# Routing of a four-batch chunk cut into pieces, rows normed ahead of the copy, and, in the last part, reciprocal roots on VectorE and an expert product behind the transposes

## Chip, core and metric

One core of a Trainium2 chip runs the whole program in one launch. The metric is device time in microseconds (us), the median over runs of the same program. PE is TensorE, PEld its weight loads, DVE is VectorE, ACT is ScalarE, POOL is GpSimd, SP is SyncE; SP, ACT and POOL also issue DMAs.

## What is computed

Inputs are x (64 batches of 256 rows of 256 floats), one 256x256 adjacency matrix, and the weights of two layers. All is float32.

```python
x = x + elu(attention_of_4_heads(layernorm(x), adj, W0, a0))   # _L0_gnn_ref
x = x + layernorm(x) @ weight.T + bias                          # _L0_ffn_ref
x = x + relu(attention_of_1_head(layernorm(x), adj, W1, a1))   # _L1_gnn_ref
x = x + moe(layernorm(x))                                       # _L1_ffn_ref: 8 experts, the best 2 of each row
```

In `_moe` the eight logits of a row choose two experts and two weights; the result is the normed row itself plus, for both experts, weight x (gelu(row @ w1 + b1) @ w2 + b2). `_layernorm` needs one reciprocal root per row; there are four norms.

## The kernel before

Each batch is one Python generator, `batch_layers`, with two tiles of 128 rows (`NT` = 2). The order of the instructions on every engine is written out by hand: a loop over *ticks* (`step`) at the end of the kernel resumes every live generator once per tick, in the order of the rank that it gave with `yield` the last time (lower first); a negative rank means "go on in this same tick at that rank". A new batch starts every third tick (`TICKS` = 3), so a tick has a phase 0, 1 or 2, about six batches are in flight, and the engines see in each phase a fixed mix of stages of different batches. All engines run their own queue in order.

In the first 61 batches (`ROUTED`) the expert layer is routed. `CHUNKS` has twelve chunks of four batches, then five of two and three of one; the last three batches are dense (all eight experts). When the last batch of a chunk has its logits (`pl`, L701, rank 35 in phase 2), `route` runs for the chunk: `top_two` (the two best experts, 13 small DVE operations with `m`, L1026), a pair of tiny matmuls that count rows ahead (`pp`, L1034 and L1035), a scan and positions (`both` to `pos`, L1037 to L1063), the two weights (L755 to L758), and then one tick after another the indirect DMAs that send each row to its place (`send`, L1000, on POOL, two per tick), with `allot` between them, which hands out pairs of tiles to experts. `later` waits for a phase. After the last send the chunk's pairs are put in `waiting`.

A *pair* (`expert_pair`) is 256 rows of one expert: loads (`xr`, `xt`, `we`), a transpose on DVE (`sT`, L117), `hidden` (`ph`, L892 on PE, then Gelu, L898 on ACT), `result` (`py`, L907 on PE, then L917 on DVE), a scaling (L885 on ACT), and two indirect DMAs that add the rows to the output (`scatter`, L928, on POOL). Up to the tick `DRAIN_AT` = 3 x 59 = 177 two pairs are begun in phase 1 of every batch; from there on (batch 59 starts) one pair per tick.

Norms: `norm_stats` (DVE, L375 and L376; the norms of x0 and x1) and `norm_squares` (ACT, L402; the two norms of x2) give variances; `finish_norms` and `finish_squares` take the root for up to four columns at once with two POOL operations, an add (L383, L412) and a power (L384, L415). The norm ahead of the experts makes `by` on DVE (L659, L662) in phase 0, rank 8, from the root of the tick before; then, at rank 50, ACT writes the normed rows `xng` (L671) and `base` (L676). `xng` is turned by PE (`pt`, L421) at rank 55 of phase 1 for the logits. `transposed` is four PE transposes and one ACT copy (`xT`, L427). Ranks that matter below: phase 0: 20 `projected1` (`pq`, L472), 22 `projected` (L437), 30 `transposed(x1)`, 31 an ACT-queue DMA (L579) that waits for a DVE transpose; phase 1: 25 `scores1` (`pd`, L491), 50 `attended` (`pv`, L544), 70 `pf` (L618) and x2 (L625); phase 2: 7 `norm_squares(x2)`, 30 a pair's `hidden`, 35 `pl`, 36 `transposed(x2)`, 40 `attended` of the single head.

Of the kernel before, what the change touches and what calls it, by code (L numbers as in the profile page):

```python
# [27 lines left out]
def kernel(  # L28
# [17 lines left out]
    nc = tc.nc  # L46
    B, N, D = x.shape
# [311 lines left out]


    half_done = []

    def norm_stats(src):

# [13 lines left out]
            finish_norms(2 * NT)  # L378
        return mv[:, at : at + NT, :], rstd[:, at : at + NT]

    def finish_norms(n):
        mv, rstd = half_done.pop()
        nc.gpsimd.tensor_scalar_add(rstd[:, :n], mv[:, :n, 1], EPS)  # L383
        nc.gpsimd.tensor_tensor(rstd[:, :n], rstd[:, :n], mhalf[:, :n], ALU.pow)  # L384

# [4 lines left out]

    def norm_squares(src, sums):
        if half_squared:
            sq, rstd = half_squared[0]
            at = NT
        else:
            sq = small.tile([P, 2 * NT], F32, tag="sq", name="sq", bufs=4)
            rstd = small.tile([P, 2 * NT], F32, tag="rstd", name="rstd", bufs=5)
            half_squared.append((sq, rstd))
            at = 0
        for t in range(NT):  # L400
            off = work.tile([P, D], F32, tag="off", name="off", bufs=1)
            nc.scalar.activation(  # L402
                off, src[:, t, :], AF.Square, bias=sums[:, t : t + 1], scale=-float(D),
                accum_out=sq[:, at + t : at + t + 1],
            )
        if at:
            finish_squares(2 * NT)
        return rstd[:, at : at + NT]

    def finish_squares(n):  # L410
        sq, rstd = half_squared.pop()
        nc.gpsimd.tensor_scalar(  # L412
            rstd[:, :n], sq[:, :n], 1.0 / D**3, EPS, op0=ALU.mult, op1=ALU.add
        )
        nc.gpsimd.tensor_tensor(rstd[:, :n], rstd[:, :n], mhalf[:, :n], ALU.pow)  # L415
# [138 lines left out]
    def batch_layers(b, c0, xng, lg):  # L554
# [105 lines left out]
            by[:, 0], sums, -1.0 / D, rstd, op0=ALU.mult, op1=ALU.mult  # L660
        )
        nc.vector.tensor_scalar(by[:, 1], rstd, 1.0, None, op0=ALU.add)  # L662
        yield -50
        xe = keep.tile([P, NT, ROW], F32, tag="xng", name="xng", bufs=XNG)
        dense = b >= ROUTED
        base = (
# [3 lines left out]
        for t in range(NT):  # L670
            nc.scalar.activation(  # L671
                xe[:, t, :D], x2[:, t, :], AF.Identity, bias=by[:, 0, t : t + 1],
                scale=rstd[:, t : t + 1],
            )
        for t in range(NT):
            nc.scalar.activation(  # L676
                base[:, t, :], x2[:, t, :], AF.Identity, bias=by[:, 0, t : t + 1],
                scale=by[:, 1, t : t + 1],
            )
# [44 lines left out]
    def chunk_tile(shape, name, c, bufs=2, dt=F32):  # L724
        return keep.tile([P] + shape, dt, tag=name, name=f"{name}_{c}", bufs=bufs)

    def top_two(c, nt, lg, first):


        rt = lambda shape, name: chunk_tile(shape, name, c)  # L730
        vec, tt = nc.vector, nc.vector.tensor_tensor
        emb = em8[:, None, :].to_broadcast([P, nt, E])
        ohs, tops, lcur = rt([2, nt, E], "ohs"), [], lg
        for k in range(2):
            top = rt([nt], f"top{k}")
            vec.tensor_reduce(top, lcur, AX.X, ALU.max)
            eq = rt([nt, E], "eq")
            tt(eq, lcur, top[:, :, None].to_broadcast([P, nt, E]), ALU.is_equal)
            tt(eq, eq, emb, ALU.mult)

            least = rt([nt], "least") if k else first
            vec.tensor_reduce(least, eq, AX.X, ALU.min)
            oh = ohs[:, k]
            tt(oh, emb, least[:, :, None].to_broadcast([P, nt, E]), ALU.is_equal)
            if k == 0:
                lcur = rt([nt, E], "l2")
                vec.scalar_tensor_tensor(lcur, oh, -3.0e38, lg, op0=ALU.mult, op1=ALU.add)
            tops.append(top)
        ed = rt([nt], "ed")
        tt(ed, tops[1], tops[0], ALU.subtract)  # L750
        return ohs, ed

    def two_weights(less, second, ed):

# [15 lines left out]
    def allot(c, n, last):  # L770

        rt = lambda shape, name, bufs=2, dt=F32: chunk_tile(shape, name, c, bufs, dt)
        vec, tt = nc.vector, nc.vector.tensor_tensor
        full = rt([E], "full")
        vec.tensor_scalar(
            full, rows[0], 1.0 / PAIR, ((PAIR - 1.0 if last else 0.0) - (PAIR - 1.0) / 2) / PAIR,
            op0=ALU.mult, op1=ALU.add,
        )  # L780
        whole(full, full)
        wait = rt([E], "wait")
        tt(wait, full, used, ALU.subtract)
        ends = rt([E], "ends")
        vec.tensor_tensor_scan(ends, ones[:, :E], wait, 0.0, ALU.mult, ALU.add)
        start = rt([E], "start")
        tt(start, ends, wait, ALU.subtract)
        tt(shift[:, :E], used, start, ALU.subtract)
        took = rt([E], "took")
        vec.tensor_scalar(took, start, -1.0, float(n), op0=ALU.mult, op1=ALU.add)  # L790
        vec.scalar_tensor_tensor(took, took, 0.0, wait, op0=ALU.max, op1=ALU.min)
        tt(used, used, took, ALU.add)
        step = rt([E], "step")
        tt(step, shift[:, 1:], shift[:, :E], ALU.subtract)
        yield
        past = rt([n, E], "past")
        tt(
            past, ends[:, None, :].to_broadcast([P, n, E]),
            jrow[:, :n, None].to_broadcast([P, n, E]), ALU.is_le,
        )  # L800
        ef = rt([n], "ef", 8)
        vec.tensor_reduce(ef, past, AX.X, ALU.add)
        ids = rt([2, n], "ids", 8, I32)
        vec.tensor_scalar(ids[:, 0], ef, float(E - 1), None, op0=ALU.min)
        vec.tensor_scalar(ef, ef, float(E - 1), float(-E), op0=ALU.min, op1=ALU.add)
        tt(past, past, step[:, None, :].to_broadcast([P, n, E]), ALU.mult)
        pair_of = rt([n], "pair_of")
# [10 lines left out]
    def expert_pair(j, n, ids, ef, regs, needs):  # L818
# [46 lines left out]
        xT = turned(work.tile([P, KT, PAIR], F32, tag="sT", name="sT", bufs=3), xr)  # L865
        w = small.tile([P, 2], F32, tag="w", name="w", bufs=12)
        yield 30
        yield 30
        hT = hidden(xT, we)
        yield -65  # L870
        nc.vector.scalar_tensor_tensor(
# [121 lines left out]
        active.append([rank, len(order), job])  # L993
        order.append(job)

    order, order_steps = [], []

    def send(xe, at):

        d = nc.gpsimd.indirect_dma_start(  # L1000
# [10 lines left out]
    def later(rank, *phases):  # L1011

        yield rank
        while more and order_steps[-1] % TICKS not in phases:
            yield rank

    def route(c, row0, nt, n, last, xng, lg):

        rt = lambda shape, name, bufs=2, dt=F32: chunk_tile(shape, name, c, bufs, dt)
        vec, tt = nc.vector, nc.vector.tensor_tensor  # L1020
        yield -90

        tail = rt([nt, 3], "tail")
        ohs, ed = top_two(c, nt, lg, tail[:, :, 0])
        m = rt([E, nt], "m")
        tt(m.rearrange("p e t -> p t e"), ohs[:, 0], ohs[:, 1], ALU.add)  # L1026


        spread = nt == NTC
        yield from later(90, *((0,) if spread else (1, 2)))  # L1030

        mf = m.rearrange("p e t -> p (e t)")
        pp = bank("pp", [2, E, nt])
        nc.tensor.matmul(pp[:, 0].rearrange("p e t -> p (e t)"), tri, mf, start=True, stop=True)  # L1034
# [26 lines left out]
        vec.tensor_reduce(posf, ohs, AX.X, ALU.add)  # L1061
        pos = rt([2, nt], "pos", 4, I32)
        vec.tensor_copy(pos, posf)  # L1063
        yield from later(90, *((0,) if spread else (1, 2)))
        two_weights(tail[:, :, 1], tail[:, :, 2], ed)
        for i, xe in enumerate(xng):
            vec.tensor_copy(xe[:, :, D + 1 :], tail[:, i * NT : (i + 1) * NT, :])
        parts = allot(c, n, False)
        if n and not spread:
            next(parts)  # L1070
            ids, ef = next(parts)
        if last:
            ends_at = rt([E], "ends_at", 2, I32)
            vec.tensor_copy(ends_at, rows[0])
# [2 lines left out]
        for t in range(nt):  # L1077
            for k in range(2):
                send(xng[t // NT][:, t % NT, :], pos[:, k, t : t + 1])
            if n and spread and t in (1, 4):  # L1080
                ids, ef = next(parts) or (None, None)
            if not last:
                yield 95
            elif t % 2:
                yield 95
# [5 lines left out]
            )  # L1091
        if last:
            parts = allot(c + 1, FLUSH, True)
            next(parts)
            ids2, ef2 = next(parts)
# [23 lines left out]
    def route_dense(b, lg):  # L1119

        c = len(CHUNKS) + 1 + b - ROUTED
        ohs, ed = top_two(c, NT, lg, chunk_tile([NT], "first", c))
        yield 75
        nc.scalar.activation(ed, ed, AF.Exp)
        two = chunk_tile([2, NT], "two", c)
# [40 lines left out]
    step, more, credit = 2, True, 0.0  # L1166


    DRAIN_AT = TICKS * (B - 5)
    SETUP_AT = 4  # L1170
    dense_free = 0
    with tc.manual_schedule():
        while more or active or waiting or dense_jobs or scatters:
# [35 lines left out]
            if half_done:  # L1209
                finish_norms(NT)  # L1210
            if half_squared:
                finish_squares(NT)
            active[:] = [a for a in active if a[0] is not None]
            step += 1

# [34 lines left out]
```

## Time and profile before

| | |
|---|---|
| median of 3 runs | 1548.69 us (1545.79 to 1563.14) |
| the profiled execution | 1561.7 us, of which the span of the instructions is 1559.9 us |
| PE, PEld busy | 93%, 82% of the span |
| DVE, ACT, POOL busy | 80%, 65%, 56% |
| mean granted TensorE clock | 0.963 |

The span has three parts. Up to about 311 us there are batches but (almost) no pairs. From about 368 to 1068 us four batches and eight pairs together take 82 us. The last part starts with tick 177, at about 1140 us (first norm of batch 59); the last batch's first norm is at 1238.9 us, the routing of the last batches ends near 1400 us, and from there pairs and dense experts alternate on PE. A line of the view by windows gives, for one stretch of time, its length, the busy time and number of instructions of PE, PEld, DVE, ACT and POOL, the granted share of the PE clock, and the share and rate of the DMA engines. A line of the waits gives engine and line that waited, what ended the wait, the total us, how often, and the longest.

### The profile page before, as it was taken

Reading aid. Unit: us, or ns where it says so; the run is one execution under the profiler, and the core shown is the slowest. Engines: PE = TensorE matmul, PEld = TensorE weight load, DVE = VectorE, ACT = ScalarE, POOL = GpSimd, SP = SyncE. Lnnn points to the kernel's source line nnn. Section 1 sums busy time; section 2 is a strip of 40 time slices with the busy share of each in tenths; the row PEclk is TensorE's granted clock in tenths of the full one; section 3 lists DMA queues with packets and bytes.
Section 4 is the critical chain, followed back from the end, with each engine's and each line's share of the span. In section 5 each row is a group of like instructions: output and inputs, shape, how many; then the busy total and the mean of one; then the engine's idle time right before and its main releaser. Section 6 shows DMA issues by size and latency. Waiting matters only on the chain. (4 is left out here: it accounts for less than half of the span.)

```text
span 1559.9 us, 29960 instructions
## 1 busy us (share of the span) xinstructions
PE 1457.4 (93%) x8066; PEld 1283.5 (82%) x8066; DVE 1252.9 (80%) x4392; ACT 1006.7 (65%) x2381; POOL 878.1 (56%) x853
## 2 busy tenths in 40 slices
PE   7899998899999999999999999999898988869997
PEld 6688887788888989898989898888787867757886
DVE  7787879798898988888888888889888868545544
ACT  1365556577777777777777777766676778644332
POOL 2111435356666767575767575766764667644443
PEclk9888889899999999999999999999999999989999
DMA  5653333367777778777877777777677776788863
GB/s 148 201 150 90 110 104 109 108 171 156 184 173 171 171 164 181 164 181 157 193 163 184 161 179 164 169 160 183 156 168 165 146 159 126 148 192 157 158 106 46
DMA packets 372851, 240.83 MB, mean 154 GB/s; under 512 B 264772, under 2 KB 334924, under 8 KB 372684
## 3 DMA queue, kind: packets, MB, share of 16 engines
q1 hardware_dynamic: 311488, 138.31, 36.3%
q0 software_dynamic: 48864, 66.33, 23.5%
q10 hardware_dynamic: 12332, 34.28, 6.7%
q8 instruction: 66, 1.08, 0.3%
q14 instruction: 101, 0.83, 0.2%
HBM read 150.46 MB, written 88.35 MB: 153 GB/s over the span
## 5 line engine op out<-in xcount | busy, mean ns | idle before, releaser
L928 POOL DMA_INDIRECT out_dram<-y,xt x258 | 413.7, 1604 | 197.5 <-issue 69.3
L544 PE MATMUL pv<-q,z 128*128 128x65 f32 (+1 forms) x2560 | 375.7, 304 | 0.3
L544 PEld LDWEIGHTS pv<-q,z 128*128 128x128 f32 x2560 | 343.5, 200 | 12.9 <-DVE z L530 0.8
L1000 POOL DMA_INDIRECT xs<-xng,pos x244 | 260.0, 1065 | 65.7 <-issue 59.3
L907 PE MATMUL py<-w2s,hT 128*128 (+1 forms) x1224 | 287.6, 386 | 8.6 <-ACT hT L898 8.5
L907 PEld LDWEIGHTS py<-w2s,hT 128*128 128x128 f32 x1224 | 232.6, 194 | 42.8 <-ACT hT L898 11.7
L892 PE MATMUL ph<-sT,we 128*128 128x256 f32 x1032 | 242.0, 383 | 8.0 <-DMA we<-wpack 2.3
L530 DVE SCALAR_TENSOR_TENSOR z<-z,q,mask 128x256 f32<-128x256 f32 x504 | 232.3, 482 | 13.4 <-DMA z<-terms 4.4
L892 PEld LDWEIGHTS ph<-sT,we 128*128 128x128 f32 x1032 | 196.1, 192 | 38.6 <-PE ph L892 5.3
L671 ACT ACTIVATE xng<-x,by,rstd 128x256 f32<-128x256 f32 x128 | 69.8, 593 | 156.4 <-DVE stats L375 82.2
L898 ACT ACTIVATE hT<-ph,we 128x256 f32<-128x256 f32 x306 | 123.4, 472 | 64.4 <-PE ph L892 47.3
L885 ACT ACTIVATE y<-y,w 128x256 f32<-128x256 f32 x258 | 112.0, 497 | 80.9 <-DVE y L917 79.3
L383 POOL TENSOR_SCALAR rstd<-mv 128x4 f32<-128x4 f32 (+1 forms) x67 | 15.9, 238 | 252.5 <-DVE mv L376 200.5
L472 PE MATMUL pq<-wx,xT 128*128 128x259 f32 x512 | 129.2, 395 | 26.3 <-ACT xT L427 26.2
L427 ACT COPY xT<-pt 128x512 f32<-128x512 f32 x192 | 113.8, 592 | 43.4 <-PE pt L421 43.4
L402 ACT ACTIVATE off<-x,sums 128x256 f32<-128x256 f32 x256 | 129.4, 505 | 17.6 <-DVE x L625 11.9
L472 PEld LDWEIGHTS pq<-wx,xT 128*128 128x128 f32 x512 | 96.5, 194 | 53.2 <-ACT xT L427 39.4
L618 PE MATMUL pf<-wfT,xT 128*128 128x256 f32 x512 | 133.8, 409 | 0.0
L917 DVE TENSOR_TENSOR y<-py,b2s 128x512 f32<-128x512 f32 x129 | 85.8, 686 | 55.9 <-PE py L907 42.1
L437 PE MATMUL pq<-wx,xT 128*128 128x268 f32 x512 | 128.8, 395 | 1.9 <-DVE xT L117 1.4
L437 PEld LDWEIGHTS pq<-wx,xT 128*128 128x128 f32 x512 | 98.4, 193 | 21.3 <-DVE wx L166 1.3
L618 PEld LDWEIGHTS pf<-wfT,xT 128*128 128x128 f32 x512 | 101.2, 208 | 12.9
(164 smaller groups left out, 2380.1 us busy)
## 6 DMA issues: line engine op xcount, KB each, us to landing
we<-wpack SPq DMA_DIRECT2D x145, 288.0 KB
xr<-xs SPq DMA_DIRECT2D x516, 64.0 KB
z<-terms ACTq DMA_DIRECT2D x63, 512.0 KB
xblk<-in_x_dram SPq DMA_DIRECT2D x256, 64.0 KB
xin<-in_x_dram SPq DMA_DIRECT2D x64, 256.0 KB
out_dram<-base SPq DMA_DIRECT2D x61, 256.0 KB
out_dram<-y,xt POOLq DMA_INDIRECT x258, 4.2
xs<-xng,pos POOLq DMA_INDIRECT x244, 4.0
```

The source lines that it names most:

```text
L402: nc.scalar.activation(off, src[:, t, :], AF.Square, bias=sums[:, t : t + 1], scale=-float(D), accum_out=sq[:, at + t : at + t + 1],)
L427: nc.scalar.copy(dst, pt)
L437: nc.tensor.matmul(pq.rearrange("p h c -> p (h c)"), xT[:, k, t * P : (t + 1) * P], wx[:, k, :], start=(k == 0), stop=(k == KT - 1),)
L472: nc.tensor.matmul(pq, xT[:, k, t * P : (t + 1) * P], wx1[:, k, :], start=(k == 0), stop=(k == KT - 1),)
L530: nc.vector.scalar_tensor_tensor(z[:, j, :, h, :], terms, q[:, j, h, HD + 2 : HD + 3], masks[0][:, j, :].rearrange("p (t i) -> p t i", t=N ...
L544: nc.tensor.matmul(pv[:, h, :], z(j, h, t), q[:, j, h, : d + 1], start=(j == 0), stop=(j == NT - 1),)
L618: nc.tensor.matmul(pf[:, t, :], xT[:, k, t * P : (t + 1) * P], wfT[:, k, :], start=(k == 0), stop=(k == KT - 1),)
L892: nc.tensor.matmul(ph[:, f, :], we[:, k * D + f * P : k * D + (f + 1) * P], xT[:, k, :], start=(k == 0), stop=(k == KT - 1),)
L898: nc.scalar.activation(hT[:, f, :], ph[:, f, :], AF.Gelu, bias=we[:, C_B1 + f : C_B1 + f + 1])
L907: nc.tensor.matmul(py[:, t, :], hT[:, f, t * P : (t + 1) * P], w2s[:, e, f * D : (f + 1) * D].rearrange("p e c -> p (e c)"), start=(f == 0 ...
L928: d = nc.gpsimd.indirect_dma_start(out=out_rows, out_offset=bass.IndirectOffsetOnAxis(ap=xt[:, t, 0:1].bitcast(I32), axis=0), in_=y[:, t, ...
L1000: d = nc.gpsimd.indirect_dma_start(out=xs_d[: E * CAP * PAIR, :], out_offset=bass.IndirectOffsetOnAxis(ap=at, axis=0), in_=xe, in_offset=None,
```

## The change

`top_two` and `allot` become generators that stop once more in the middle, and `route` for chunks of four takes its pieces in fixed ticks in place of `later`; other chunks run them through with `in_one`. With s for the tick of the logits (phase 2), a chunk of four before had `top_two` in s, `pp` to `pre` in s+1, `pos` in s+3, the weights in s+4, sends in s+5 to s+12. After: half of `top_two` in s+1, the rest and `m` in s+2, `pp` in s+3 at rank 41, the copy and scan in s+4, positions and weights in s+5, sends in s+6 to s+13, and four steps of `allot` in place of two among them. The normed rows `xng` go from rank 50 to rank 29, `base` stays at 50. From tick `DRAIN_AT` on, the roots are made on DVE (`inverse_root`: a first guess from the bits, and three Newton steps, ten operations, behind one for the variance), those of `norm_squares` at the end of the tick; and a pair's `hidden` that falls in phase 2 goes from rank 30 to rank 37.

```diff
+    DRAIN_AT = TICKS * (B - 5)
+    order, order_steps = [], []
...
+    def draining():
+        return order_steps[-1] >= DRAIN_AT
+
+    def inverse_root(y, v):
+
+        n = v.shape[-1]
+        t = small.tile([P, 2 * NT], F32, tag="root", name="root", bufs=2)[:, :n]
+        nc.vector.tensor_scalar(
+            y.bitcast(I32), v.bitcast(I32), -0.5, float(0x5F3759DF), op0=ALU.mult, op1=ALU.add
+        )
+        for _ in range(3):
+            nc.vector.tensor_tensor(t, y, y, ALU.mult)
+            nc.vector.scalar_tensor_tensor(t, t, -0.5, v, op0=ALU.mult, op1=ALU.mult)
+            nc.vector.scalar_tensor_tensor(y, t, 1.5, y, op0=ALU.add, op1=ALU.mult)
+
     def finish_norms(n):
         mv, rstd = half_done.pop()
+        if draining():
+            var = small.tile([P, 2 * NT], F32, tag="sq", name="var", bufs=4)[:, :n]
+            nc.vector.tensor_scalar(var, mv[:, :n, 1], EPS, None, op0=ALU.add)
+            inverse_root(rstd[:, :n], var)
+            return
         nc.gpsimd.tensor_scalar_add(rstd[:, :n], mv[:, :n, 1], EPS)
         nc.gpsimd.tensor_tensor(rstd[:, :n], rstd[:, :n], mhalf[:, :n], ALU.pow)
...
-        if at:
-            finish_squares(2 * NT)
+        if at and not draining():
+            finish_squares()
...
-    def finish_squares(n):
-        sq, rstd = half_squared.pop()
+    def finish_squares():
+        sq, rstd, n = half_squared.pop()
+        if draining():
+            nc.vector.tensor_scalar(
+                sq[:, :n], sq[:, :n], 1.0 / D**3, EPS, op0=ALU.mult, op1=ALU.add
+            )
+            inverse_root(rstd[:, :n], sq[:, :n])
+            return
...
-        yield -50
+        yield -29
         xe = keep.tile([P, NT, ROW], F32, tag="xng", name="xng", bufs=XNG)
...
+        yield -50
         for t in range(NT):
             nc.scalar.activation(
                 base[:, t, :], x2[:, t, :], AF.Identity, bias=by[:, 0, t : t + 1],
...
                 vec.scalar_tensor_tensor(lcur, oh, -3.0e38, lg, op0=ALU.mult, op1=ALU.add)
+                yield
...
         tt(wait, full, used, ALU.subtract)
+        yield
         ends = rt([E], "ends")
...
         vec.tensor_scalar(ef, ef, float(E - 1), float(-E), op0=ALU.min, op1=ALU.add)
+        yield
         tt(past, past, step[:, None, :].to_broadcast([P, n, E]), ALU.mult)
...
-        yield 30
+        yield 37 if draining() and order_steps[-1] % TICKS == 1 else 30
         hT = hidden(xT, we)
...
-        yield -90
-
+        spread = nt == NTC
+        if spread:
+            yield 90
+        else:
+            yield -90
         tail = rt([nt, 3], "tail")
-        ohs, ed = top_two(c, nt, lg, tail[:, :, 0])
+        parts = top_two(c, nt, lg, tail[:, :, 0])
+        if spread:
+            next(parts)
+            yield 90
+        ohs, ed = in_one(parts)
...
-        spread = nt == NTC
-        yield from later(90, *((0,) if spread else (1, 2)))
+        if spread:
+            yield 41
+        else:
+            yield from later(90, 1, 2)
...
         nc.tensor.matmul(pp[:, 1].rearrange("p e t -> p (e t)"), ones, mf, start=True, stop=True)
+        if spread:
+            yield 90
         both = rt([2, E, nt], "both")
...
         if spread:
-            yield from later(90, 2)
+            yield 90
...
-        yield from later(90, *((0,) if spread else (1, 2)))
+        if not spread:
+            yield from later(90, 1, 2)
...
-            if n and spread and t in (1, 4):
+            if n and spread and t in (1, 2, 4, 5):
                 ids, ef = next(parts) or (None, None)
```

More of the change, by code (lines that the diff above doesn't have):

```diff
@@ L392, in norm_squares @@
         if half_squared:
-            sq, rstd = half_squared[0]
-            at = NT
+            sq, rstd, at = half_squared.pop()
         else:
@@ L397, in norm_squares @@
             rstd = small.tile([P, 2 * NT], F32, tag="rstd", name="rstd", bufs=5)
-            half_squared.append((sq, rstd))
             at = 0
+        half_squared.append((sq, rstd, at + NT))
         for t in range(NT):
@@ L725, in chunk_tile, with in_one @@
         return keep.tile([P] + shape, dt, tag=name, name=f"{name}_{c}", bufs=bufs)
+    def in_one(parts):
+        got = None
+        for got in parts:
+            pass
+        return got
     def top_two(c, nt, lg, first):
@@ L750, in top_two @@
         tt(ed, tops[1], tops[0], ALU.subtract)
-        return ohs, ed
+        yield ohs, ed
     def two_weights(less, second, ed):
@@ L994, in begin @@
         order.append(job)
-    order, order_steps = [], []
     def send(xe, at):
@@ L1069, in route @@
         if n and not spread:
-            next(parts)
-            ids, ef = next(parts)
+            ids, ef = in_one(parts)
         if last:
@@ L1093, in route @@
             parts = allot(c + 1, FLUSH, True)
-            next(parts)
-            ids2, ef2 = next(parts)
+            ids2, ef2 = in_one(parts)
             _, ends_sp = nc.values_load_multi_w_load_instructions(
@@ L1121, in route_dense @@
         c = len(CHUNKS) + 1 + b - ROUTED
-        ohs, ed = top_two(c, NT, lg, chunk_tile([NT], "first", c))
+        ohs, ed = in_one(top_two(c, NT, lg, chunk_tile([NT], "first", c)))
         yield 75
@@ L1166 @@
     step, more, credit = 2, True, 0.0
-    DRAIN_AT = TICKS * (B - 5)
     SETUP_AT = 4
@@ L1211 @@
             if half_squared:
-                finish_squares(NT)
+                finish_squares()
             active[:] = [a for a in active if a[0] is not None]
```

## The prediction

> **What bounds the kernel now.** First the page's busy shares: PE 93%, DVE 80%. So a gain has to come out of PE's idle time or of a slow PE clock, and the granted clock is 0.963 over the span. By windows of 40 us PE is idle 12 of the 720 us from 360 to 1080, so that part is bound by PE. The losses lie before and behind it, and they are different ones.
>
> *The early part*, by windows around one routing. The columns are length, busy us of PE, PEld, DVE, ACT, POOL, then the clock.
>
> ```profile
> core 0: us, PE busy (x) PEld busy (x) DVE busy (x) ACT busy (x) POOL busy (x), PEclk, DMA share, GB/s
> ...
> 195.00:209.60 14.60, 14.60 (x95) 13.02 (x93) 13.17 (x48) 8.91 (x26) 8.32 (x11) 1.00 0.43 128
> 209.60:213.10 3.50, 0.05 (x1) 0.00 (x0) 3.16 (x16) 2.05 (x7) 0.93 (x1) 0.88 0.21 76
> 213.10:225.90 12.80, 12.75 (x53) 12.01 (x54) 6.46 (x28) 4.38 (x11) 1.38 (x3) 0.50 0.46 117
> 226.00:230.00 4.00, 4.00 (x24) 3.56 (x24) 3.82 (x10) 1.68 (x5) 1.77 (x2) 1.00 0.33 91
> ```
>
> PE is idle for 3.5 us, and for the 12.8 us behind it its clock is half. DVE, busy 90% before, is then busy 6.46 of 12.80: it waits for PE. The waits of 85 to 311 us name the stall, and the timeline of its end says the same:
>
> ```profile
> PE pp L1034 <- DVE m L1026: 10.5, 3, 3.5
> PEld pt L421 <- ACT xng L671: 8.6, 13, 2.3
> ```
>
> ```profile
> 212.82 0.27 DVE L1026 TENSOR_TENSOR m<-ohs 128x64 f32<-128x64 f32 x1
> ...
> 213.15 0.69 PE L1034 MATMUL pp<-m,tri 128*128 128x64 f32 x2 [3.50 <-DVE m L1026]
> ```
>
> `top_two` occupies DVE from 209.99 to 213.09, in one go, while PE has nothing else in its queue ahead of `pp`. It happens three times, at 138.5, 209.6 and 281.8 us, once for each early chunk. By the starts of the first norms, batches without routing are 13.8 us apart (99.6 to 127.2); from the second stall on, four batches take 17.0, 21.1, 16.9 and 17.2 us.
>
> *The last part*, by its waits (1115 to 1412 us):
>
> ```profile
> DVE by L659 <- POOL rstd L415: 24.2, 4, 9.7
> ...
> PEld pq L472 <- ACT xT L427: 17.0, 9, 3.5
> DVE x L625 <- POOL rstd L384: 13.3, 3, 7.0
> ```
>
> The roots are ready late, though a root takes about 1 us: POOL has scatters and sends ahead of it. The longest, in the timeline:
>
> ```profile
> 1363.78 0.96 POOL L1000 DMA_INDIRECT xs<-xng,pos  x1 [0.30 <-issue]
> 1365.05 1.62 POOL L928 DMA_INDIRECT out_dram<-y,xt  x1 [0.30 <-issue]
> ...
> 1368.88 0.72 POOL L415 TENSOR_TENSOR rstd<-rstd,mhalf 128x2 f32<-128x2 f32 x1
> ...
> 1369.63 0.16 DVE L659 SCALAR_TENSOR_TENSOR by<-sums,rstd 128x2 f32<-128x2 f32 x1 [9.73 <-POOL rstd L415]
> ...
> 1370.48 1.19 PE L421 MATMUL pt<-ident,xng 128*128 128x128 f32 x4 [6.13 <-ACT xng L671]
> ```
>
> From 1200 to 1411 us PE's gaps over 0.4 us add up to 35 us, and half-clock stretches in it to 31 us, which cost another 15.
>
> **The change, part by part.**
>
> *Routing in pieces (twelve chunks).* `pp` goes to phase 2 behind the single head's matmuls. The last half of `top_two` stands on DVE right behind x2 (L625) and lasts 1.5 us; PE must transpose x2 (0.65 us) and do eight matmuls (1.9 us) before it comes to `pp`, so `m` is ready about 1.0 us early. If that cover were short, the stall would be the missing part of 1 us, not 3.5. Where does DVE's 3.1 us go? One half to the end of phase 0, one to the end of phase 1, where DVE now waits for `pf` (17.9 us in 11 waits of the early part). Gain for each early chunk: the 17.0 and 21.1 us batches would come to about 16 us, the value of the next ones (16.0, 16.9, 17.2) less their waits for `xng`. That is 6 us, and 18 us for three. Low bound 3 x 4 = 12 (only the 21.1 against 17). High bound: DVE has 12.6 us of work in a batch without routing (two batches, 12.62 and 12.63) and some 9.7 for a chunk's routing (from the starts of its operations: `top_two` 3.1, `both` to `pre` 1.1, positions 0.9, weights and their copies 1.2, `allot` 3.4, as at 1354.07 to 1357.45), so 4 x 12.6 + 9.7 = 60 us instead of 72: 3 x 10 = 30 with small stalls. I take 18, nearer the low end since the waits behind the bulge have other causes.
> How much half clock hangs on a stall: by the clock's record 13.65 us behind each 3.5 us of idling, and 10.2 us behind a gap of 1.8 us (at 180.6), so 6.8 us of PE's capacity for each of the three stalls. The Trainium skill ("TensorE: Matmul & The Clock Gate", Part 1) says that the clock halves after an idle window of about 3.4 us and comes back after about one busy window; by it a stall would cost 1.7 us, and the gap of 1.8 us nothing, an estimate that the rows contradict.
>
> *Rows normed ahead.* `xng` (two ACT operations, 1.09 us) leaves its place behind the ACT-queue DMA L579, where it waits with it, and goes ahead of the copy of x1's transposes. That copy and L579 come 1.1 us later, which hides in ACT's gap there (2.36 us at 575.68). `xng` is 2.9 us earlier. The waits of `pt` for it are 6.5 us on PE in the early part, inside the sum above; in the middle part it and the routing together can give at most PE's 12 us of idle time there, and cost some 8 again where L579 comes late. I take 4.
>
> *Two pairs later.* Each chunk's last send is a tick later, in phase 1 instead of 0, so `waiting` misses that phase's start and its pairs begin three ticks later. Two more pairs are left for the last part, where PE has no slack from 1420 us on: 2 x 3.45 us (two groups of eight matmuls, 1.73 each) = 6.9 us. Against it, the batch at 308 us (18.4 us with its first two pairs) gets some 2.4 us shorter, and the end loses two ticks without a pair, with two gaps of 0.6. So 3 us lost; bounds 0 and 7.
>
> *Roots on DVE.* 18 groups, so 198 new DVE operations and 36 fewer on POOL. No row has this chain; the nearest are the weights' small dependent operations: 0.16 to 0.17 us long, 0.20 apart (1353.20, .39, .59, .79). One root is 11 x 0.20 = 2.2 us, against 1.3 to 1.4 us for four columns on POOL when it is free. All 18 take 40 us of DVE. Of it, fourteen roots or 31 us fall between 1139 and 1320 us (POOL's powers stand at 1141 to 1313), a stretch where, by windows from 1115 on, DVE is busy 169 of 205 us: it fits only barely, and behind it are the scores `z` and the weights of the pairs. From 1320 on DVE is nearly idle. The removed waits: 24.2 + 13.3 us on DVE, of which PE feels the gaps at 1275 (4.3), 1331 (1.3), 1346 (1.7), 1364 (6.1), 1383 (2.4) and 1391 us (2.7), 18.5 in all, and some 8 of clock loss.
> The Trainium skill speaks against this ("VectorE: DVE Perf Modes", Rules for kernel authors): keep the number of chained DVE operations small, as each pays its fixed term, which it gives as about 150 cycles, 0.156 us. By it the 198 would be 31 us, an estimate; the rows say 40.
>
> *`hidden` behind the transposes.* Now Gelu with its table load (1.28 + 0.84 us) stands ahead of x2's copy on ACT, and PE waits for the copy at L472: 2.2, 2.2, 3.1, 2.4 and 1.8 us from 1200 us on, 11.7 us. Afterwards Gelu follows the copy: about 2.1 us less each, 9 us. The product it covered moves between the transposes and the head's matmuls, so nothing is lost unless x2 is late; then up to 1 us for each of 9 batches.
>
> Together the last part could give 18 + 8 + 9 = 35 us. Of that I take 16, because the DVE time is close to full until 1320 us and one wait taken away lets the next show. Bounds: -35, and +10 if 10 of the 31 us find no slack and the waits give nothing back.
>
> **Sum**: -18 - 4 + 3 - 16 = -35 us against the profiled execution: 1561.7 - 35 = 1526.7. That execution is 13.0 us above the median. I take half of this to lie in the very stalls that go away, so the median goes to about 1520 (1548.69 - 28.5).
>
> **Rivals.**
> *The last part gives nothing.* DVE takes over as the bound there. For it: 41.1 of 45 us busy from 1115 to 1160. Against it: 26.2 and 16.2 of 40 in the windows at 1240 and 1360. Time: 1549 - 18 - 4 + 3 + 5 = 1535.
> *The early part gives nothing.* DVE is 95% busy in the batches around the stall (15.99 of 16.9 us), so a wait of PE may be hidden anyway, and pieces bring the same DVE work. Against it: DVE itself is idle half of the 12.8 us. Time: 1549 - 16 + 3 = 1536, and 1545 if both hold in part.
> *Slower.* The roots stand in DVE's queue in the batch's own chain (stats, root, x2; squares, root, `by`, `xng`), 2.2 against 1.3 us, and at the end of the tick behind the scores: if up to 1320 us all 31 us come on the path and the waits taken away give nothing, with 7 for the two pairs and only the 12 of the early part back: 1549 + 31 + 7 - 12 = 1575. It is slower than before once more than 5 of the 31 us stay on the path so, and by over 1% from 20 on; with 36 us of DVE slack in the windows I think that unlikely.
>
> **How the numbers follow.** Forecast 0.58 (1520, own range 1503 to 1535), last part nothing 0.20, early part nothing 0.12, slower 0.10. A difference of 1% (15.5 us, under 1533.2) is about what a measurement can tell. Faster by more: 0.55 of the forecast and half of the second case, 0.65; within 1%: 0.24; slower: 0.11, the last case and a bit of the third. The range 1492 to 1556 takes in the high early bound and the slower case's near side.
>
> **What would show it.** Right: no wait of `pp` for `m`, no half clock from 85 to 311 us, early batches near 16 us; no DVE wait for POOL's root after 1140; L472's waits under 1 us there; two more pairs behind 1420. Wrong: half clock in the early part with other gaps in front, batches still 17 us or more, DVE full from 1140 to 1320 with PE waiting for `z` or x2.

## The result, and the profile after

The changed kernel is slower: 1576.48 us in the median of 4 runs (1564.27 to 1584.53), against 1553.07 us of the kernel before in 4 runs (1545.79 to 1563.14). The ratio is 1.015, with a 95% interval of 1.0102 to 1.0197, so about 23 us. The profiled execution took 1584.53 us, its span 1582.5 us. From the page after:

```profile
span 1582.5 us, 30220 instructions
...
PE 1455.8 (92%) x8066; PEld 1285.5 (81%) x8066; DVE 1285.1 (81%) x4590; ACT 1010.9 (64%) x2379; POOL 844.9 (53%) x817
...
PEclk9999999999999999999999999999889888899997
```

The operations are as forecast (198 more on DVE, 36 fewer on POOL). The clock's row, in 40 slices, stands at 9 through the early part; it is low in the slices that hold the last part, from about 1110 to 1390 us.

**The early part did what was forecast, and more.** The two stretches that held the stall and the half clock, by windows of the kernel after (length, busy us of PE, PEld, DVE, ACT, POOL, clock):

```profile
195.00:209.60 14.60, 13.20 (x87) 11.66 (x86) 13.87 (x53) 9.51 (x26) 7.35 (x10) 1.00 0.40 115
209.60:226.00 16.40, 15.26 (x93) 12.91 (x93) 15.63 (x59) 9.61 (x27) 4.05 (x7) 1.00 0.39 107
```

The clock is 1.00 throughout, and the wait of `pp` for `m` is in no line of the waits from 85 to 311 us. Half-clock time up to 330 us falls from 75.1 to 23.9 us. Batch 22 starts (its first norm) at 336.5 us instead of 368.4. Both numbers vary from run to run: the changed kernel and the seven experiments that have the same schedule up to tick 177 (x1 to x4, x7, x8, x10) show 10.2 to 47.8 us of half clock there, and start batch 22 between 329.6 and 342.7 us; and the one profile of the kernel before is a run 9 us above the median given here.

**Then the gain goes away in three steps**, by the starts of the first norms in the two profiled executions: the lead over before is 31.9 us at batch 22, 23.5 at batch 54 (1002.1 against 1025.6), 23.0 at batch 59, 0.8 at batch 63 (1238.1 against 1238.9); at the end of the span it is a deficit of 22.6. From batch 59 to 63 alone 22.2 us are lost. The waits of the kernel after, 1115 to 1412 us (total us, times, longest):

```profile
ACT L506 <- DVE rstd L396: 35.1, 8, 7.7
...
PE pd L518 <- ACT ex L506: 21.3, 9, 5.0
...
PE pl L729 <- ACT xT L454: 15.8, 6, 4.3
```

None of these three was among the long waits there before. L506 without a tile is the table load that ACT makes ahead of the exponentials. L396 is the last operation of a root on DVE, `ex` the exponentials of the single head, `pd` their transposes on PE. The waits for POOL's roots are gone, as forecast; these took their place. The timeline of the longest wait of `pd`:

```profile
1230.82 0.71 DVE L117 STREAM_TRANSPOSE sT<-xr 128x512 f32<-128x512 f32 x1
1231.45 0.13 DVE L434 TENSOR_SCALAR sq<-sq 128x4 f32<-128x4 f32 x1
...
1233.39 0.17 DVE L396 SCALAR_TENSOR_TENSOR rstd<-root,rstd 128x4 f32<-128x4 f32 x1
1233.60 0.16 DVE L686 SCALAR_TENSOR_TENSOR by<-sums,rstd 128x2 f32<-128x2 f32 x1
1233.64 1.28 ACT L506 ACT_TABLE_LOAD   x1 [5.53 <-DVE rstd L396]
...
1234.93 0.26 ACT L506 ACTIVATE ex<-pq,rstd 128x3 f32<-128x3 f32 x1
...
1235.25 1.00 PE L518 MATMUL pd<-ident,ex 128*128 128x128 f32 x2 [5.03 <-ACT ex L506]
```

The squares' root stands at the end of DVE's tick. From 1226.4 to 1230.8 us DVE is at the small operations of the weights and of `allot`, then at a pair's transpose; only then comes the root, 2.1 us long. ACT has nothing ahead of `ex` and stands still for 5.53 us; the table load of the exponentials, 1.28 us, waits with it and is paid after the root (in the kernel before it ran ahead of such a wait; rows in the last section). PE is idle for 5.03 us, and the clock's record shows half clock for 13.7 us from 1234.7 on, with PE busy 13.11 of the 13.20 us from 1235.2 to 1248.4.

### The profile page after: what moved, and what is told of

It is laid out like the page before. It is cut to its first block, busy times and chain, and to the rows that moved or that the text cites. A ratio compares the mean times of both kernels' runs of the same rounds, so it can differ in the third digit from the quotient of the medians.

```text
span 1582.5 us, 30220 instructions
## 1 busy us (share of the span) xinstructions
PE 1455.8 (92%) x8066; PEld 1285.5 (81%) x8066; DVE 1285.1 (81%) x4590; ACT 1010.9 (64%) x2379; POOL 844.9 (53%) x817
## 4 chain that ended last, share of the span: by engine, by line
PE 53%; DVE 23%; ACT 9%; DMA 7%; issue 4%; POOL 2%; SPq 1%; DVEq 0%; ACTq 0%; POOLq 0%
PE pv L571 12%; PE py L945 12%; PE ph L930 11%; DVE z L557 5%; PE pf L645 4%; PE pq L464 4%; PE pq L499 4%; PE pt L448 3%; DMA xr<-xs 2%; DMA terms<-ut 1%; PE pl L729 1%; DVE x L652 1%; ACT hT L936 1%; ACT L506 1%; DVE x L634 1%
## 5 line engine op out<-in xcount | busy, mean ns | idle before, releaser
L571 PEld LDWEIGHTS pv<-q,z 128*128 128x128 f32 x2560 | 343.2, 200 | 13.2 <-DVE z L557 0.6
L1036 POOL DMA_INDIRECT xs<-xng,pos x244 | 255.7, 1048 | 71.0 <-issue 59.7
L945 PE MATMUL py<-w2s,hT 128*128 (+1 forms) x1224 | 280.2, 380 | 4.8 <-ACT hT L936 4.8
L945 PEld LDWEIGHTS py<-w2s,hT 128*128 128x128 f32 x1224 | 229.2, 191 | 36.0 <-ACT hT L936 7.2
L930 PE MATMUL ph<-sT,we 128*128 128x256 f32 x1032 | 254.9, 399 | 3.8 <-DVE sT L117 2.9
L930 PEld LDWEIGHTS ph<-sT,we 128*128 128x128 f32 x1032 | 205.4, 202 | 34.3 <-DVE sT L117 3.3
L499 PE MATMUL pq<-wx,xT 128*128 128x259 f32 x512 | 130.8, 399 | 23.7 <-ACT xT L454 23.4
L499 PEld LDWEIGHTS pq<-wx,xT 128*128 128x128 f32 x512 | 96.9, 195 | 46.3 <-ACT xT L454 32.7
L671 ACT ACTIVATE rel<-pv,rinv 128x256 f32<-128x256 f32 x128 | 53.6, 468 | 123.2 <-DVE rinv L578 123.2
L645 PE MATMUL pf<-wfT,xT 128*128 128x256 f32 x512 | 125.8, 390 | 0.0
L464 PEld LDWEIGHTS pq<-wx,xT 128*128 128x128 f32 x512 | 101.2, 198 | 23.2 <-DVE xT L117 1.3
L117 DVE STREAM_TRANSPOSE sT<-xr 128x512 f32<-128x512 f32 x129 | 87.9, 700 | 23.0 <-DMA xr<-xs 21.6
```

The costliest lines, as they stand in the source:

```text
L464: nc.tensor.matmul(pq.rearrange("p h c -> p (h c)"), xT[:, k, t * P : (t + 1) * P], wx[:, k, :], start=(k == 0), stop=(k == KT - 1),)
L499: nc.tensor.matmul(pq, xT[:, k, t * P : (t + 1) * P], wx1[:, k, :], start=(k == 0), stop=(k == KT - 1),)
L571: nc.tensor.matmul(pv[:, h, :], z(j, h, t), q[:, j, h, : d + 1], start=(j == 0), stop=(j == NT - 1),)
L645: nc.tensor.matmul(pf[:, t, :], xT[:, k, t * P : (t + 1) * P], wfT[:, k, :], start=(k == 0), stop=(k == KT - 1),)
L930: nc.tensor.matmul(ph[:, f, :], we[:, k * D + f * P : k * D + (f + 1) * P], xT[:, k, :], start=(k == 0), stop=(k == KT - 1),)
L945: nc.tensor.matmul(py[:, t, :], hT[:, f, t * P : (t + 1) * P], w2s[:, e, f * D : (f + 1) * D].rearrange("p e c -> p (e c)"), start=(f == 0 ...
```

## The experiments

The kernels without an edit of the last part show the same batches without that loss, so the edits were taken apart. Times are medians; ratios are to the kernel before, on the same chip, with 95% intervals. "B59 to B63" is the time from the first norm of batch 59 to that of batch 63 in the profiled execution: 99.3 us before, 121.5 after.

### First four: the last part taken apart

**x1: routing in pieces and rows at rank 29; both edits of the last part off.**

```diff
     def finish_norms(n):
         mv, rstd = half_done.pop()
-        if draining():
+        if False:
...
-        if at and not draining():
+        if at:
             finish_squares()
...
         sq, rstd, n = half_squared.pop()
-        if draining():
+        if False:
...
-        yield 37 if draining() and order_steps[-1] % TICKS == 1 else 30
+        yield 30
```

> The change without its two edits for the last part: roots on POOL, a pair's product at rank 30; routing in pieces, normed rows at rank 29 and the two late pairs stay. Theory A (the late root): the squares' root on DVE stands at the end of the tick behind scores and routing, and ex with its table load and PE's pd wait for it; then the last part is as before, the early gain of 32 us stays less 10 in the middle and some 5 for the late pairs: 15 to 20 us faster than before, 0.988. Theory B (the product's place): the same here. Theory C (late pairs and the scatter chain at the end): the end stays late, 0.995 to 1.005 of before, and the last scatter comes over 10 us after the last matmul.

Measured: 1543.24 us (1537.91 to 1551.92), ratio 0.9954 (0.9923 to 0.9985). B59 to B63 takes 100.0 us. So the loss of 22 us is the last part's edits, and the first two edits bring something, but far less than the starts of the early batches promise: a lead of 37.8 us at batch 22 (330.6) ends as 6 in the median.

**x2: roots on POOL again, product left at rank 37.**

```diff
     def finish_norms(n):
         mv, rstd = half_done.pop()
-        if draining():
+        if False:
...
-        if at and not draining():
+        if at:
             finish_squares()
...
         sq, rstd, n = half_squared.pop()
-        if draining():
+        if False:
```

> The change with all roots on POOL, the pair's product still at rank 37 in phase 2. Theory A: as fast as without both edits or some 5 us faster, since pq waits less for the copy of x2: 0.985 to 0.99 of before; pd's waits for ex under 5 us in all. Theory B: PE's waits of pl for the copy of the normed rows (15.8 us in the changed kernel) stay, and it is 10 us or more slower than the kernel without both edits.

Measured: 1549.29 us, ratio 0.9997 (0.9977 to 1.0017), 6.0 us more than x1. The waits from 1092 to 1412 us, of x1 and then of x2:

```profile
PE pq L499 <- ACT xT L454: 15.1, 8, 3.5
...
PE pl L729 <- ACT xT L454: 3.3, 2, 2.5
```

```profile
PE pl L729 <- ACT xT L454: 16.5, 6, 4.3
```

In x2 the wait of `pq` is off the list, as forecast, and that of `pl` has grown by the same amount. The product at rank 30 filled PE while ACT copied the turned `xng` for the logits; moved behind, it fills the next wait and uncovers this one. The 6 us come back wherever this edit is the only difference: x3 against the changed kernel 0.36%, x10 against x4 (below) 0.44%, here 0.43%; each pair's intervals touch, the three agree. Where they lie in the span is not shown: B59 to B63 is still 100.0 us, and from there to the end it is 333.6 us against 332.2; 5.6 of the 6.9 us by which the two profiles differ stand ahead of batch 59, where the two run the same schedule.

**x3: roots on DVE, product back at rank 30.**

```diff
-        yield 37 if draining() and order_steps[-1] % TICKS == 1 else 30
+        yield 30
```

> The change with roots on DVE, but the pair's product at rank 30 as before. Theory A: no better than the changed kernel, 1.01 to 1.02 of before, and PE's pd still waits 20 us for ex. Theory B: 12 to 16 us faster than the changed kernel, 1.003 of before, and pl's waits for the copy gone.

Measured: 1563.35 us, ratio 1.0114 (1.0045 to 1.0182), 20 us more than x1. B59 to B63: 118.6 us. The wait of x3 that x1 doesn't have:

```profile
ACT L506 <- DVE rstd L396: 34.8, 8, 7.2
```

**x4: the changed kernel, with the squares' root between the two halves of the scores `z` in place of the end of the tick.**

```diff
         yield -70
+        if draining() and half_squared:
+            finish_squares()
         scores(q, z, range(2, 4), b > 0)
```

> The change with one thing moved: the squares' root on DVE not at the end of the tick, but between the two halves of the scores in phase 2, some 8 us earlier in DVE's queue; the same operations. Theory A: pd's waits for ex fall from 21 us to under 5, and 10 to 20 us come back against the changed kernel (1.00 of before or under). A rival (DVE is simply too full, 40 us of new work): no change, within 4 us of the changed kernel.

Measured: 1563.4 us, ratio 1.0085 (1.0051 to 1.0118), B59 to B63 111.5 us. The number and kind of the operations are those of the changed kernel; the waits of `ex` for the root fall from 35.1 to 8.2 us in all, those of `pd` from 21.3 to 4.1. So 0.65% (10 us by ratios, 13 by medians; the two intervals just touch) is the place of the squares' root alone, not its operations.

### Second four: which edit wins, and which root loses

**x5: routing in pieces alone** (x1 with the rows behind the copy again). **x6: the rows at rank 29 alone**, on the kernel before. The diff is x5's; x6 makes the same move the other way.

```diff
-        yield -29
+        yield -50
         xe = keep.tile([P, NT, ROW], F32, tag="xng", name="xng", bufs=XNG)
...
-        yield -50
         for t in range(NT):
             nc.scalar.activation(
                 base[:, t, :], x2[:, t, :], AF.Identity, bias=by[:, 0, t : t + 1],
```

> The early part's gain halved: the routing of a chunk of four is in pieces as in the changed kernel, the normed rows stay behind the copy at rank 50, both edits of the last part are off. Theory R (the wait of the prefix matmul behind one long stretch of VectorE work was the early loss, and the rows' place costs the middle its 2.1 us gap a chunk): the start of batch 38 stays some 25 to 30 us ahead of before's, the gaps at the projection behind the copy in the middle go away, and the time is 1530 to 1540. Rival X (the rows ahead of the copy bring the early gain): batch 38 is level with before's within 8 us and the time is 1550 to 1558, since the pairs that begin three ticks later cost the end some 5 us.

> Before with the normed rows at rank 29 alone, everything else as before. Theory R: no early gain, the middle loses about 2 us a chunk, the time is 1553 to 1562, against about 1550 of before. Rival X: 1535 to 1545 with batch 38 more than 15 us ahead of before's.

Measured: x5 1536.06 us, ratio 0.9927 (0.99 to 0.9954), batch 38 36.7 us ahead of before's; x6 1542.49 us, ratio 0.9962 (0.9937 to 0.9987), batch 38 13.5 us ahead. Each wins alone, and routing brings nearly all of the early gain. Yet together (x1, 0.9954) they are no better than either. A likely reason shows in PE's gaps ahead of the projection `pq` (L499 here): from 385 to 966 us they are 2.0 to 2.3 us once in every chunk in x1, 0.6 to 1.1 us in x5, and in x6 there are only two, of 0.9 and 1.7 us. The theory's forecast that rows alone would lose was wrong.

**x7** was meant to put the two late pairs back (below), but its edit let an `elif` take over the yield that it dropped:

```diff
-            if not last:
+            if not last and not (spread and t == nt - 1):
                 yield 95
             elif t % 2:
                 yield 95
```

> As the kernel with both edits of the last part off (1543.24 median, last scatter 16.1 us behind its y), but the last of a chunk's six yields behind a send is dropped, so that the pairs that a chunk fills are counted in the tick in which they could be counted before the change. Theory C (two pairs more for the end, at 3.5 us a pair, and their scatters one behind the other, cost 5 to 8 us): the time is 1535 to 1539 and the last scatter starts within 12 us of its y. Rival (the pairs of the last part run in ticks that have room for them, so that the end doesn't notice): 1542 to 1545.

It is the same program as x1, so it says nothing of the pairs. Its 1543.53 us against 1543.24 shows how well the medians repeat; its profiled span is 1549.0 us against 1542.1, with 34.1 us of half clock up to 330 us against 10.2. One profile alone can't settle 7 us.

**x8: x1, with only the layer norms' roots on DVE** (those of the squares on POOL).

```diff
     def finish_norms(n):
         mv, rstd = half_done.pop()
-        if False:
+        if draining():
```

> Routing and rows as changed, product at rank 30, and of the two kinds of reciprocal roots of the last part only those of the layer norms by VectorE; those of the squares stay with GpSimd. It stands between the kernel with all roots on GpSimd (1543.24) and the one with all on VectorE (1563.35). Theory A (the loss is the squares' root, which stands at the end of VectorE's tick with the exponentials behind it): 1538 to 1546, and the waits of the exponentials at L506 are below 12 us in all. Rival (the nine dependent VectorE operations of a root cost the same wherever they stand, because VectorE is itself what the last part waits for): 1551 to 1556, half of the difference.

Measured: 1545.98 us, ratio 0.9988 (0.996 to 1.0015), 2.7 us above x1 and 17 below x3; B59 to B63 103.0 us. The wait at L506 for a root on DVE is gone. The norms' roots are the same eleven operations each, eight of the eighteen; their 2.7 us are inside the intervals. So of the 20 us that roots on DVE cost, nearly all comes with the squares' ten (which without the norms' were not run).

### Last four: the two late pairs

A chunk's pairs begin three ticks late in the changed kernel because its last send moved from phase 0 to phase 1. One yield behind that send, dropped properly, puts them back: the schedule then starts the last pair in tick 222 as before, not 224.

```diff
             if not last:
-                yield 95
+                if not (spread and t == nt - 1):
+                    yield 95
             elif t % 2:
```

**x9**: that, on x5. **x11**: that, on x1. **x12**: that, on the changed kernel. **x10**: the changed kernel with the early root of x4 and the product back at rank 30 of x3.

> The routing in pieces alone (1536.06 median), and the yield behind a chunk's last send dropped: the schedule then lists a chunk's pairs one tick earlier, in phase 0, and they begin in the tick after it, as before the change, so that 222 is again the last tick in which a pair begins (224 with the change). Theory C (the two pairs that are left over for the end cost what two pairs take there, 6.9 us each at the pace of the last pairs, less what they had hidden): 1524 to 1530, and the time from the start of batch 63 to the last y falls from 301.4 us to about 290. Rival (the end is set by the chain of scatters, which has the same 129 pairs to land): 1534 to 1538.

> The changed kernel with both repairs of the last part: the squares' root on VectorE stands between the two halves of the scores, and the expert product is back at rank 30. If the two losses add (27 us of late roots, of which the place gave 13 back, and 6 us of the product): 1555 to 1559. If the product's place costs only where the exponentials are late too: 1561 to 1565.

> Routing in pieces and rows at rank 29, no edit of the last part (1543.24 median), with a chunk's pairs back in the tick in which they began before. Theory: the middle's gap of 2.0 to 2.3 us ahead of the first layer's projection, once a chunk, is there because the copy of the turned rows stands behind a table load and four Gelus of a pair that begins three ticks later than before; with the pairs back it shrinks to the 0.7 to 1.7 us of the kernels that have one of the edits, and the time is 1530 to 1534, both from this and from the end. Rival: the gap comes of the rows' place alone and stays above 2 us; the time is then 1535 to 1538, from the end alone.

> The whole changed kernel, with a chunk's pairs back in the tick in which they began before (one yield dropped). If the delay of the pairs costs what it costs without the edits of the last part (1543.24 less 1522.03, 21 us), the time is 1553 to 1558 against 1576.48 of the changed kernel, and what is left above 1522 is the late roots and the product's place, 33 us. If the late pairs and the late roots hide each other in the last part, where both delay the same products: 1563 to 1570, with the middle's part of it alone gained.

Measured:

| | median us | ratio | 95% interval |
|---|---|---|---|
| x9: routing, pairs back | 1527.02 | 0.9836 | 0.9796 to 0.9875 |
| x11: routing and rows, pairs back | 1522.03 | 0.9822 | 0.9775 to 0.9868 |
| x12: the whole change, pairs back | 1558.06 | 1.0012 | 0.9988 to 1.0036 |
| x10: early root, product at 30, pairs late | 1558.8 | 1.0041 | 1.0008 to 1.0075 |

x9 is inside what the delay's theory gave, and its last `y` comes 287.1 us after the start of batch 63, against 301.4 in x5; x12 is at its theory's upper edge; x11 is 8 us below it, with the gaps ahead of `pq` at 0.6 to 1.6 us as expected. x10 is what it should be if the two losses of the last part add: against x3, which differs in the root's place alone, 0.73% less by ratios, as x4 against the changed kernel, though only 4.6 us by medians, and the intervals touch. Its waits, 1092 to 1412 us:

```profile
ACT L506 <- DVE rstd L396: 8.1, 3, 3.0
...
PE pd L518 <- ACT ex L506: 2.0, 4, 1.4
```

So the early place gives back 5 us (medians) to 11 us (ratios) of the 17 to 20 us of the squares' root, x3 less x8. It does not give all: B59 to B63 is 109.7 us in x10 and 103.0 in x8, and what the rest waits for was not taken further. The table load behind the root (last section) is a candidate that no run separates.

Four of these ratios form a square, which is the account of the whole change:

| | pairs on time | pairs late |
|---|---|---|
| without the last part's edits | 0.9822 | 0.9954 |
| with them | 1.0012 | 1.0150 |

Late pairs cost 1.32% in one row and 1.38% in the other, some 21 us; the last part's edits cost 1.90% and 1.96%, some 30 us. Within the intervals (0.2 to 0.5% to either side) neither depends on the other. Without the rows' edit the delay looks cheaper: from x5 to x9 it is 0.91%, 14 us (9 by medians). So some of the 21 us may belong to the delay and the rows' place together; the intervals don't tell 0.91 from 1.32%. The other two edits, with the pairs on time, bring 1.8%, 28 us. So -28 + 21 + 30 = 23 us, the result.

x11 beats both kernels, the one before by 1.8% and the changed one, by the ratios, by 3.2%.

Where the 21 us of the pairs lie, x1 against x11, 24.0 us apart in span: x1 is 4.2 us ahead at batch 22, then loses 13.2 us in the middle, takes 2.5 back to batch 63, and loses 17.5 behind it. In the middle (batch 22 to 54) x1 takes 664.9 us and x11 651.7. The waits from 372 to 1050 us, x1 first:

```profile
PE pq L499 <- ACT xT L454: 17.0, 8, 2.3
```

```profile
PE pq L499 <- ACT xT L454: 5.0, 10, 1.6
```

and one of the eight in x1's timeline:

```profile
466.44 1.28 ACT L936 ACT_TABLE_LOAD   x1
...
467.73 1.57 ACT L936 ACTIVATE hT<-ph,we 128x256 f32<-128x256 f32 x4
469.18 0.60 ACT L454 COPY xT<-pt 128x512 f32<-128x512 f32 x1
...
469.83 2.58 PE L499 MATMUL pq<-wx,xT 128*128 128x259 f32 x8 [2.11 <-ACT xT L454]
```

A pair's Gelu with its table load is on ACT ahead of the copy that PE waits for. Once a chunk, DVE waits some 2 to 3 us for a pair's rows (`sT` for `xr`: eight waits of at most 2.8 us in x1, 2.0 in x11), and it may be that everything behind is late by that, and that with late pairs this falls where PE runs out of work. That the gaps need the delay is shown by x11, and that they need the rows' place too by x5, whose pairs are as late and whose middle is 656.3 us (653.9 in x9); why this phase is the worse one was not taken further.

At the end, by windows from the last pair's `y` to the end of the span, x1 and then x11:

```profile
1516.00:1542.00 26.00, 11.15 (x48) 8.46 (x47) 7.39 (x16) 2.52 (x6) 9.67 (x7) 0.82 0.37 56
```

```profile
1491.50:1518.00 26.50, 18.60 (x80) 14.34 (x79) 11.09 (x24) 4.20 (x10) 9.36 (x7) 0.95 0.37 55
```

Behind the last `y` both need 26 us, with 48 matmuls left for PE or 80. In x1 the chain that ended last goes through the queue of scatters. In x11 the scatters and the dense experts end nearly together: the last scatter's instruction ends at 1511.5 us, the last dense sum on DVE at 1515.1, and the chain goes through the dense experts. So what makes the difference is when the last `y` comes: 306.1 us after the start of batch 63 in x1, 288.1 in x11. In that stretch x1 does 961 matmuls of experts, x11 897. The 64 are two pairs and two units of the dense experts, 16 each, that alternate with them; in x11 those two units run beside the last scatters. Up to its last `y` PE is busy 11.4 us longer in x1 and idle 32.6 against 26.0 us.

## Why the prediction was wrong, step by step

*Routing in pieces*: right in mechanism, a little small in size. It took 18 us "nearer the low end" of 12 to 30; x9 shows 22 us in the median. The 31.9 us at batch 22 of the changed kernel are against the one profile of the kernel before, a run above its median. The half clock went with the stalls, 51 us less of it in the two profiles; how much of the gain that is was not separated. The Trainium skill ("TensorE: Matmul & The Clock Gate", Part 1) lets the clock come back after about one busy window of 3.4 us; the runs side with the rows, since in the changed kernel too the record shows 13.7 us of half clock from the end of a gap of 5.03 us on, with PE busy in it.

*Rows ahead*: forecast 4 us. x6 gives 0.4% (6 us); on top of routing 1522.03 against 1527.02 us, whose intervals overlap, so not told apart from nothing. With the pairs late it turns: x1 is 7 us slower than x5 by medians.

*Two pairs later*: forecast +3 with a bound of 7; measured 21. **This step failed in its price and its place.** It counted the two pairs' own matmuls, 2 x 3.45 us, as if PE's work set the end. The last pair's `y` sets it, and it comes two ticks later, of 6.9 us each at that pace, with a dense unit in each: 14 of the 18 us, an estimate (64 matmuls where the sum had 32). And it took the middle for untouched by the delay; there it cost 13 us together with the rows' new place.

*Roots on DVE*: **this is the step that turned the sign.** The last part as a whole was put at -16 us, with +10 as the far bound; it was +30. The bound was made from DVE's slack (36 us in the windows), as if a root cost only when DVE is full. (It also took DVE for nearly idle from 1320 us on; the windows before show it busy 26.32 of the 40 us to 1360.) By windows from batch 59 to 63, after and x1:

```profile
1116.60:1238.10 121.50, 101.41 (x501) 86.86 (x501) 99.65 (x404) 73.19 (x162) 53.37 (x45) 0.89 0.65 140
```

```profile
1109.90:1209.90 100.00, 90.93 (x499) 79.45 (x498) 84.71 (x316) 74.11 (x163) 61.67 (x57) 0.98 0.75 165
```

DVE is busy 99.65 of 121.50 us, not full. PE does the same 500 matmuls; it is idle 20.1 us instead of 9.1 and takes 10.5 us longer for them at a clock of 0.89. So it is latency rather than a full engine: a root on DVE's queue stands behind all that the tick has put there, and on POOL it ran beside it. The forecast named both facts ("2.2 against 1.3 us, and at the end of the tick behind the scores") but only in the rival, and there it priced the operations' 31 us. x8 shows that eight of the eighteen roots, with the same operations, cost 2.7 us, which the intervals don't tell from nothing, and x4 and x10 that the place is a good part of the price of the others, 10 to 13 us in one and 5 to 11 in the other. That the rival's 1575 us is close to the result is luck: its sum has 12 us for the early part and 7 for the pairs, where 28 and 21 were measured. The table load behind a late root, 1.28 us each time, was in no term of the sum either.

*Product behind the transposes*: forecast 9 us gained; the three comparisons show 6 lost. The wait of `pq` went away as priced. The sentence "nothing is lost unless x2 is late" missed `pl`, which stands on the line between: the product had been its cover too.

*The profiled execution against the median*: half of its 13 us was put to the stalls. x7 bears out that such differences lie there: the same program differed by 7 us of span, with 24 us more half clock in the early part.

## What to carry to other kernels

Before moving work to another in-order engine, look up what stands ahead of it there in the same tick and who waits for its result: busy shares and the number of operations would have passed this move, its place in the queue did not. When a step is delayed by one tick, ask which start it now misses, and price it at the pace of whatever ends last, not at its own work. And when a wait is filled with work from elsewhere, name the wait that this work filled until now.

## What was not expected of the hardware

The table load ahead of an exponential can stand behind the wait for that exponential's operand. In the changed kernel ACT stood still for 5.53 us and then took 1.28 us for the load, 0.08 us after the root's end at 1233.56; all eight waits of the load for a root, 35.1 us, are of this kind. In the kernel before, with the root on POOL, the load ran first and only the exponential waited:

```profile
1205.60 1.28 ACT L479 ACT_TABLE_LOAD   x1
1209.98 0.26 ACT L479 ACTIVATE ex<-pq,rstd 128x3 f32<-128x3 f32 x1 [3.10 <-POOL rstd L415]
```

So the move to DVE also put 1.28 us behind each of the eight late roots, some 10 us of ACT in all (an estimate; no run separates it from the root's place). What decides on which side of the wait the load stands was not isolated. The Trainium skill ("ScalarE: Activation LUTs", What ACT_TABLE_LOAD costs) gives 1283 ns for a load, as the rows here do; that it can lengthen a wait in this way is what the timeline adds.

The scatters that add to the output follow one another at 6.2 to 6.8 us a pair at the end (7.1 once in x11 and x12), hardly faster than pairs are made there (6.9 us). A backlog that they bring along is therefore hardly worked off before the last `y`: the first scatter of the last pair starts 10.3 us after it before, 16.1 in x1, 16.6 in x11, 17.2 in x12, 24.1 in the changed kernel. What makes the backlog was not isolated.
